# Linear attention with half of its key products moved to GpSimd, and cosine keys one step after their turning

## The chip, the core and the metric

The kernel runs on one core of a Trainium2 chip. The core has five engines that run side by side and wait for each other through semaphores: TensorE (PE in the profile, its weight loads PEld), VectorE (DVE), ScalarE (ACT), GpSimd (POOL) and SyncE (SP), which here issues DMAs. Each engine works off its own instructions in a fixed order. Tiles lie in SBUF or in PSUM; TensorE writes to PSUM, and GpSimd's operands in this kernel are all in SBUF. The metric is the device time of one execution in microseconds (us), the median of several runs.

## The reference, cut to what matters

The model has two layers of three blocks each, on x of 4 sequences x 512 positions x 256 channels, all in float32. Two blocks matter here. Cosine attention (16 heads of 128, one key and value head shared by all):

```python
xn = _layernorm(x, g_norm)
q = xn @ Wq
kv = xn @ Wkv
k, v = (kv[..., :DIM_HEAD], kv[..., DIM_HEAD:])
...
k = _l2norm(k)
...
sim = jnp.einsum('bhid,bjd->bhij', q, k)
attn = jax.nn.softmax(sim.astype(jnp.float32), axis=-1).astype(sim.dtype)
out = jnp.einsum('bhij,bjd->bhid', attn, v)
```

and gated linear attention (16 heads, 8 key channels and 16 value channels each):

```python
def step(S, inp):
    qt, kt, vt, gt = inp
    S = S * jnp.exp(gt)[..., None] + kt[..., None] * vt[..., None, :]
    ot = jnp.einsum('bhk,bhkv->bhv', qt, S)
    return (S, ot)
...
_, o = jax.lax.scan(step, S0, (qT, kT, vT, gT))
...
o = o * jax.lax.rsqrt(jnp.mean(o * o, axis=-1, keepdims=True) + EPS) * norm_w
o = o * (g * jax.nn.sigmoid(g))
return o.reshape(b, t, vd) @ Wo
```

## The kernel before, in words

The blocks follow each other, with parts of neighbouring blocks woven in. TensorE's order is that of the source; the order on the other engines was made when the program was built, by a planner that places each engine's instructions in advance.

**Cosine attention** (`cos`, some 537 to 1310 us of the span) goes over 16 batches, four heads of one sequence each, and within a batch over four steps k. Step k of batch n holds two `scores` (8 matmuls and an exponential), `values` (8 matmuls, a copy of the result, and the sum of the exponentials, part of it on GpSimd, line 726), and, at fixed (n, k), the preparation of what comes next. The next sequence is prepared by `enter`: at (1, 3) its layer norm, and at (2, 1) both `turned` (8 transposes on TensorE, then two scaled copies by VectorE, line 605, into `own_xt`) and, straight after, `keys` (16 matmuls on `own_xt`, then copies and the norm of the keys). At step (3, 1) of the same sequence the keys are transposed (`turn`, line 635).

**Linear attention** (`gla_stage`, `run`, some 1313 to 1490 us) lays out each state on partitions: one partition for a key channel of a head, time along the row. So the recurrence over time is one scan instruction of VectorE per value channel, with the decay as the factor. For a sequence b and a step n of four (`steps`, 16 in all), `states` handles two pairs of value channels, pair 0 and 1. For a pair:

- TensorE spreads the values over the partitions into `pv`, a PSUM tile of two banks with two buffers (line 932);
- VectorE multiplies by the keys in place, in PSUM (line 933, the *key product*);
- VectorE scans each half into `st` in SBUF (line 936), reading decay from SBUF and product from PSUM;
- GpSimd multiplies by the queries into another SBUF tile, `sq` (line 941, the *query product*); only the very last one of the stage is VectorE's.

`reads`, held back by one step, sums the query products over the key channels on TensorE (line 951) into an accumulator `po`, one for every two steps; there are two accumulator buffers in this stage. When one is complete, ScalarE squares it (959) and copies it to SBUF (963), and after the second GpSimd multiplies both by the gate (965). For the last sequence VectorE multiplies the accumulator by the gate directly (961). `output` then makes the norm and projects.

Woven into the stage are the preparation of the next sequence (`prepare`), the last feed-forward block (`extra`: a chain of small VectorE instructions, lines 517 to 540), and the folding of later weights (1087 to 1119), whose vectors GpSimd prepares (1063 to 1079) when their DMA has landed.

Of the kernel before, what the change touches and what calls it, by code (L numbers as in the profile page):

```python
# [9 lines left out]
F32 = mybir.dt.float32  # L10
I32 = mybir.dt.int32
U32 = mybir.dt.uint32
AF = mybir.ActivationFunctionType
ALU = mybir.AluOpType
AX = mybir.AxisListType

P = 128
# [8 lines left out]
class Model:  # L26
# [559 lines left out]
    def cos(self, w, woven):  # L586
# [4 lines left out]
        with self.pool("cos_2", 2) as p2:  # L591

            def normed(b):
                if b == 0:
                    return self.xn_first
                xn = p2.tile([P, NI, D], F32, name="cxn", tag="cxn", bufs=1)
                self.doubly(xn, b)
                return xn

            def turned(xn):  # L600
                xt = p2.tile([P, NC, T], F32, name="own_xt", tag="own_xt")

                def gained(dst, pt):
                    for c in range(NC):
                        nc.vector.tensor_scalar_mul(dst[:, c, :], pt[:, c, :], w["gn"][:, c : c + 1])

                self.turned(xn, xt, gained)
                return xt
# [33 lines left out]
                    self.b, self.h0 = n // NB, n % NB * 4  # L642

            bs = [Batch(n) for n in range(B * NB)]
            seq = {}

            def project(t, pair):
# [120 lines left out]
            def enter(b, part):  # L768
                if part == 0:
                    seq[b] = {"xn": normed(b)}  # L770
                else:
                    s = seq[b]
                    s["xt"] = turned(s["xn"])
                    s["k"], s["v"] = keys(s["xt"])

            if True:
                enter(0, 0)
                enter(0, 1)
                project(bs[0], 0)
                project(bs[0], 1)  # L780
                query_norms(bs[0])
                seq[0]["kt"] = turn(seq[0]["k"])
                project(bs[1], 0)
                project(bs[1], 1)
                spread_rows(bs[0].rn, bs[0].q)
                for n, t in enumerate(bs + [None]):
                    nxt, then = (bs[n + d] if n + d < len(bs) else None for d in (1, 2))
                    prev = bs[n - 1] if n else None
                    for k in range(4):
                        if prev and t and k == 0:  # L790
                            sums(prev)
                        if t:
                            scores(t, k, 0)
                            scores(t, k, 1)
                        if t and t.b + 1 < B and (n % NB, k) in ((1, 3), (2, 1)):
                            enter(t.b + 1, k == 1)
                        if n and nxt and k == 0:
                            project(nxt, 1)
                        if then and k == 3:
                            project(then, 0)  # L800
                        if nxt and k == 1 and nxt.h0 == 0:
                            seq[nxt.b]["kt"] = turn(seq[nxt.b]["k"])
                        if prev and not t and k == 1:
                            sums(prev)
                        if prev and k == 2:
                            if t:
                                scaled(prev.o, prev.wide, t.put)
                            else:
                                spread_rows(prev.rd, prev.o)
                        if t:  # L810
                            values(t, k)
                        if nxt and k == 0:
                            query_norms(nxt)
                        if nxt and k == 2:
                            scaled(nxt.q, nxt.sq, t.put)
                        if prev and k == (2 if t else 3):
                            output(prev)
                        if (n, k) in woven:
                            next(woven[n, k], None)
# [27 lines left out]
    def gla_stage(self, w):  # L847
# [64 lines left out]
        def run(order, extra, p2, p3):  # L912
# [9 lines left out]
            def states(b, n, pair):  # L922

                s = seqs[b]
                c, odd = n // 2, n % 2
                q = s.qk[:, 0, :].unsqueeze(1).to_broadcast([P, 2, T])
                k = s.qk[:, 1, :].unsqueeze(1).to_broadcast([P, 2, T])
                pv = self.st()
                for m in range(2):
                    r = pair * 2 + m  # L930
                    g = slice(r * 32, (r + 1) * 32)
                    nc.tensor.matmul(pv[:, m, :], lhsT=rep[g, odd, :], rhs=s.v[g, c, :], start=True, stop=True)
                nc.vector.tensor_tensor(pv, pv, k, op=ALU.mult)  # L933
                st = p3.tile([P, 2, T], F32, name="gs", tag="gs", bufs=3)
                for m in range(2):
                    s.scan = nc.vector.tensor_tensor_scan(  # L936
                        st[:, m, :], s.dec, pv[:, m, :], 0.0, op0=ALU.mult, op1=ALU.add
                    )
                sq = p3.tile([P, 2, T], F32, name="gqs", tag="gqs", bufs=4)
                end = (b, n, pair) == (order[-1], NB - 1, 1)  # L940
                (nc.vector if end else nc.gpsimd).tensor_tensor(sq, st, q, op=ALU.mult)
                return sq

            def reads(b, n, qs):
                s = seqs[b]
                c, odd = n // 2, n % 2
                if odd == 0:
                    s.po = s.po if c else []
                    s.po.append(self.ps())
                for r in range(4):  # L950
                    nc.tensor.matmul(
                        s.po[c][r * 32 : (r + 1) * 32, :], lhsT=summ[:, odd, :], rhs=qs[r // 2][:, r % 2, :],
                        start=odd == 0, stop=odd == 1,
                    )
                if odd:
                    if c == 0:
                        s.sq = p2.tile([P, NC, T], F32, name="gsq", tag="gsq", bufs=1)
                        s.o = p2.tile([P, NC, T], F32, name="go", tag="go")
                    nc.scalar.activation(s.sq[:, c, :], s.po[c], AF.Square)
                    if b == order[-1]:  # L960
                        nc.vector.tensor_tensor(s.o[:, c, :], s.po[c], s.g[:, c, :], op=ALU.mult)
                        return
                    nc.scalar.activation(s.o[:, c, :], s.po[c], AF.Copy)
                    if c:
                        nc.gpsimd.tensor_tensor(s.o, s.o, s.g, op=ALU.mult)

            def output(b, part):
                s = seqs[b]
# [27 lines left out]
            for n, (k, m) in enumerate(steps):  # L996
                b = order[k]
                nxt = order[k + 1] if k + 1 < len(order) else None
                prev = order[k - 1] if k else None
                qs = [states(b, m, 0)]  # L1000
                if nxt is not None:
                    prepare(nxt, {0: "turned", 1: 1, 2: 2, 3: 3}[m], p2)
                if m == 1 and k > 1:
                    with self.tc.issue_after(seqs[b].scan.ins):
                        output(order[k - 2], 2)
                qs.append(states(b, m, 1))
                for g in extra.get(n, ()):
                    next(g, None)
                if m == 0:
# [990 lines left out]
```

## Time and profile before

| | |
|---|---|
| median of 3 runs | 1987.21 us (1987.01 to 1987.48) |
| the profiled execution's own time | 1987.09 us |
| its span, first to last instruction | 1985.2 us |
| busy, whole span | PE 93%, DVE 62%, ACT 41%, POOL 36% |
| mean granted TensorE clock | 0.98 |
| first and last scan (line 936) | 1319.7 and 1467.6 us |
| first and last query product on POOL (line 941) | 1322.2 and 1463.9 us |

The costliest groups on the page with a part in the change are these (line, engine, operation, output from input, shapes and count; then busy us, mean ns of one; then idle us before them and who ended it):

```profile
L726 POOL TENSOR_TENSOR e<-e 128x1024 f32<-128x1024 f32 x64 | 155.6, 2430 | 598.8 <-ACT e L718 591.5
L253 PE MATMUL ps_two<-cq,ckt 128*128 128x512 f32 x512 | 236.6, 605 | 2.5 <-DVE cq L676 2.5
L253 PE MATMUL ps_acc<-e,cv 128*128 128x512 f32 x512 | 230.7, 593 | 1.8 <-ACT e L718 1.8
```

An instruction on a line of the timeline has its start, its duration, its engine and line, and in brackets the idle time of its engine before it with what ended that. Names say where a tile lies: those with `ps_` are in PSUM, all others in SBUF.

### The profile page before, as it was taken

How to read it: one execution, taken by the hardware profiler on the slowest of the kernel's cores; microseconds unless marked ns; L12 is line 12 of the kernel's file. 1: busy time of each engine (PE TensorE's matmuls, PEld its weight loads, DVE VectorE, ACT ScalarE, POOL GpSimd, SP SyncE). 2: the span in 40 equal slices, each digit the busy share in tenths (PEclk: the TensorE clock that was granted, in tenths of full speed). 3: DMA queues.
4: the chain of work that ended last, by engine and by line, in shares of the span. 5: the costliest groups of instructions: out<-in, count | busy, mean ns of one | idle time of the engine just before them, and what ended most of it. 6: DMA issues, size and time to landing. Idle time of an engine off the chain costs nothing.

```text
span 1985.2 us, 25536 instructions
## 1 busy us (share of the span) xinstructions
PE 1853.3 (93%) x8718; PEld 1057.8 (53%) x8718; DVE 1230.8 (62%) x2998; ACT 806.7 (41%) x1939; POOL 705.8 (36%) x710
## 2 busy tenths in 40 slices
PE   7999999999999999999999999978988869999886
PEld 4656566565644544544454554533346645666465
DVE  5676767767546546654755475278885566567454
ACT  3544545546333222323232224224423346666543
POOL 3554454544212113211321221236653235553232
PEclk9999999999999999999999999989989989999998
DMA  5020000000001112112111211110000000000001
GB/s 192 1 99 1 1 1 1 0 1 1 22 21 43 43 44 56 46 40 50 47 44 47 55 43 39 26 50 0 1 6 22 1 1 1 1 1 1 1 1 43
DMA packets 42880, 54.34 MB, mean 27 GB/s; under 512 B 12512, under 2 KB 25344, under 8 KB 42368
## 3 DMA queue, kind: packets, MB, share of 16 engines
q1 hardware_dynamic: 42752, 52.73, 10.0%
q8 instruction: 69, 1.13, 0.2%
q14 instruction: 59, 0.48, 0.1%
HBM read 19.14 MB, written 2.10 MB: 11 GB/s over the span
## 4 chain that ended last, share of the span: by engine, by line
PE 76%; DVE 13%; ACT 6%; POOL 2%; issue 2%; DMA 1%; SPq 0%; DVEq 0%; ACTq 0%; POOLq 0%
PE ps_acc L253 30%; PE ps_two L253 24%; PE ps_acc L1626 4%; PE ps_acc L446 3%; PE ps_acc L434 3%; DVE gs L936 2%; PE ps_acc L1673 2%; PE ps_acc L665 1%; PE ps_acc L1307 1%; ACT ws_junk L1352 1%; DVE ps_st L933 1%; DVE rp L161 1%; DVE ln_st L189 1%; PE ps_acc L1582 1%; DMA s16a<-in_mla_wqn 1%
## 5 line engine op out<-in xcount | busy, mean ns | idle before, releaser
L726 POOL TENSOR_TENSOR e<-e 128x1024 f32<-128x1024 f32 x64 | 155.6, 2430 | 598.8 <-ACT e L718 591.5
L271 DVE CUSTOM_DVE_ANT_0 ps_acc<-ps_acc,mask 128x128 f32<-128x128 f32 (+3 forms) x448 | 224.9, 540 | 63.6 <-PE ps_acc L1626 42.7
L718 ACT ACTIVATE e<-ps_two 128x1024 f32<-128x1024 f32 x128 | 130.5, 1021 | 292.8 <-PE ps_two L253 292.6
L253 PE MATMUL ps_two<-cq,ckt 128*128 128x512 f32 x512 | 236.6, 605 | 2.5 <-DVE cq L676 2.5
L253 PE MATMUL ps_acc<-e,cv 128*128 128x512 f32 x512 | 230.7, 593 | 1.8 <-ACT e L718 1.8
L417 POOL TENSOR_TENSOR prob<-prob,psum_row 128x256 f32<-128x256 f32 (+3 forms) x128 | 159.9, 1252 | 174.2 <-DVE psum_row L416 151.1
L412 ACT ACTIVATE prob<-ps_acc,nmax 128x128 f32<-128x128 f32 (+3 forms) x256 | 134.3, 528 | 152.8 <-DVE nmax L271 109.6
L253 PE MATMUL ps_acc<-key,q 128*128 128x256 f32 (+3 forms) x512 | 163.3, 441 | 5.9 <-POOL q L341 5.0
L253 PEld LDWEIGHTS ps_two<-cq,ckt 128*128 128x128 f32 x512 | 95.4, 192 | 130.0 <-issue 125.1
L253 PEld LDWEIGHTS ps_acc<-e,cv 128*128 128x128 f32 x512 | 96.5, 190 | 122.9 <-issue 96.9
L253 PE MATMUL ps_two<-own_xt,s16a 128*128 128x512 f32 x256 | 114.8, 592 | 0.0
L253 PE MATMUL ps_two<-s16b,cot 128*128 128x256 f32 x512 | 113.1, 379 | 0.0
L727 DVE TENSOR_TENSOR es<-e 128x512 f32<-128x512 f32 x64 | 43.9, 686 | 110.5 <-POOL e L726 110.5
L724 DVE COPY cot<-ps_acc 128x512 f32<-128x512 f32 x64 | 44.1, 689 | 104.7 <-PE ps_acc L253 104.7
L253 PEld LDWEIGHTS ps_two<-s16b,cot 128*128 128x128 f32 x512 | 97.3, 190 | 20.1 <-issue 7.7
L253 PEld LDWEIGHTS ps_acc<-key,q 128*128 128x128 f32 x512 | 83.2, 191 | 39.2 <-issue 16.9
L434 PEld LDWEIGHTS ps_acc<-ident,prob 128*128 128x128 f32 x640 | 76.6, 142 | 47.3 <-issue 37.4
L341 POOL TENSOR_TENSOR q<-rope,rope 64x512 f32<-64x512 f32 x64 | 81.1, 1267 | 49.7 <-DVE rope L338 47.0
L434 PE MATMUL ps_acc<-ident,prob 128*128 128x128 f32 x640 | 91.1, 274 | 3.8 <-ACT prob L412 2.7
L1626 PE MATMUL ps_acc<-lo_t 32*128 32x128 f32 (+3 forms) x512 | 87.1, 454 | 3.2 <-ACT lo_t L1586 3.2
L446 PE MATMUL ps_acc<-prt,kv 128*64 128x384 f32 (+3 forms) x512 | 78.4, 439 | 4.8 <-DVE prt L129 4.6
L1626 PE MATMUL ps_acc<-lo_qm,lo_t 32*128 32x384 f32 (+3 forms) x512 | 80.9, 451 | 0.7 <-DVE lo_qm L1664 0.7
(470 smaller groups left out, 3494.4 us busy)
## 6 DMA issues: line engine op xcount, KB each, us to landing
csq<-crn SPq DMA_DIRECT2D x240, 64.0 KB, 2.0
es<-crd SPq DMA_DIRECT2D x240, 64.0 KB, 2.0
x<-in_x SPq DMA_DIRECT2D x4, 512.0 KB, 7.6
s16b<-in_mla_wo SPq DMA_DIRECT2D x1, 2048.0 KB, 17.9
s16a<-in_cos_wq SPq DMA_DIRECT2D x1, 2048.0 KB, 9.1
s16b<-in_cos_wo SPq DMA_DIRECT2D x1, 2048.0 KB, 8.5
out_x<-x SPq DMA_DIRECT2D x4, 512.0 KB, 2.9
s16a<-in_mla_wqn SPq DMA_DIRECT2D x1, 1536.0 KB, 12.8
```

Of the source, the lines that this page charges most:

```text
L253: self.nc.tensor.matmul(out, lhsT=l, rhs=r, start=k == 0, stop=k == n - 1)
L271: return self.nc.vector.tensor_tensor_reduce(out=sc[:, :n], in0=sc[:, :n], in1=self.mask[:, T - n :], scale=-1.0, scalar=3.0e38, op0=ALU.a ...
L341: nc.gpsimd.tensor_tensor(dst[k][r], t1[r], t3[r], op=ALU.add)
L412: nc.scalar.activation(pr[:, k, :n], sc[k][:, :n], AF.Exp, bias=nm[:, k : k + 1], scale=-1.0, accum_out=sm[:, k : k + 1],)
L417: nc.gpsimd.tensor_tensor(pr[:, :, :n], pr[:, :, :n], sm.unsqueeze(2).to_broadcast([P, 2, n]), op=ALU.mult)
L434: nc.tensor.transpose(pt[:, k, keys], pr[:, k0 + k, keys], self.ident)
L446: nc.tensor.matmul(po[k * R : (k + 1) * R, j * P :], lhsT=s.kv[:, j, 0, :], rhs=prt[:, k, j, j * P :], start=j == 0, stop=j == NI - 1,)
L718: nc.scalar.activation(t.e[:, pair * 2 : pair * 2 + 2, :], sc, AF.Exp)
L724: t.put = nc.vector.tensor_copy(t.o[:, k, :], po)
L726: nc.gpsimd.tensor_tensor(e2, t.e[:, 0:2, :], t.e[:, 2:4, :], op=ALU.add)
L727: nc.vector.tensor_tensor(t.es[:, k, :], e2[:, 0, :], e2[:, 1, :], op=ALU.add)
L1626: nc.tensor.matmul(sc[:, col : col + n], lhsT=left, rhs=right, start=True, stop=True)
```

## The change

In cosine attention, `enter` is split in three: the layer norm at (1, 3), the turning at (2, 1), and the key projection at (2, 2), one step later. In linear attention, pair 1 of each step, except in the very last step, takes another way: ScalarE copies the spread values from PSUM into the SBUF tile `st`, GpSimd multiplies them there by the keys, and VectorE scans `st` in place. Pair 1 is issued ahead of pair 0. The query product is written in place, so `sq` is gone, and `st` has 7 buffers where the two tiles had 3 and 4. In all sequences VectorE now multiplies the accumulator by the gate straight from PSUM; ScalarE's copy and GpSimd's gate product are gone.

```diff
@@ cosine attention
+            ENTER = [(1, 3), (2, 1), (2, 2)]
...
             def enter(b, part):
                 if part == 0:
                     seq[b] = {"xn": normed(b)}
+                elif part == 1:
+                    seq[b]["xt"] = turned(seq[b]["xn"])
                 else:
                     s = seq[b]
-                    s["xt"] = turned(s["xn"])
                     s["k"], s["v"] = keys(s["xt"])
...
                 enter(0, 1)
+                enter(0, 2)
...
-                        if t and t.b + 1 < B and (n % NB, k) in ((1, 3), (2, 1)):
-                            enter(t.b + 1, k == 1)
+                        if t and t.b + 1 < B and (n % NB, k) in ENTER:
+                            enter(t.b + 1, ENTER.index((n % NB, k)))
@@ linear attention, states
-                nc.vector.tensor_tensor(pv, pv, k, op=ALU.mult)
-                st = p3.tile([P, 2, T], F32, name="gs", tag="gs", bufs=3)
+                end = (b, n) == (order[-1], NB - 1)
+                st = p3.tile([P, 2, T], F32, name="gs", tag="gs", bufs=7)
+                if pair == 0 or end:
+                    nc.vector.tensor_tensor(pv, pv, k, op=ALU.mult)
+                else:
+                    nc.scalar.copy(st, pv)
+                    nc.gpsimd.tensor_tensor(st, st, k, op=ALU.mult)
+                    pv = st
                 for m in range(2):
                     s.scan = nc.vector.tensor_tensor_scan(
                         st[:, m, :], s.dec, pv[:, m, :], 0.0, op0=ALU.mult, op1=ALU.add
                     )
-                sq = p3.tile([P, 2, T], F32, name="gqs", tag="gqs", bufs=4)
-                end = (b, n, pair) == (order[-1], NB - 1, 1)
-                (nc.vector if end else nc.gpsimd).tensor_tensor(sq, st, q, op=ALU.mult)
-                return sq
+                end = end and pair == 0
+                (nc.vector if end else nc.gpsimd).tensor_tensor(st, st, q, op=ALU.mult)
+                return st
@@ reads
-                    if b == order[-1]:
-                        nc.vector.tensor_tensor(s.o[:, c, :], s.po[c], s.g[:, c, :], op=ALU.mult)
-                        return
-                    nc.scalar.activation(s.o[:, c, :], s.po[c], AF.Copy)
-                    if c:
-                        nc.gpsimd.tensor_tensor(s.o, s.o, s.g, op=ALU.mult)
+                    nc.vector.tensor_tensor(s.o[:, c, :], s.po[c], s.g[:, c, :], op=ALU.mult)
@@ the steps of run
-                qs = [states(b, m, 0)]
+                qs = [states(b, m, 1)]
...
-                qs.append(states(b, m, 1))
+                qs.insert(0, states(b, m, 0))
```

## The prediction

> **What bounds the kernel now.** I read the busy shares first, then two stretches side by side, then the waits inside them, and last single instructions. TensorE (PE) has 93% of the whole span, but that is an average over stages.
>
> ```profile
> 520.00:1000.00 480.00, 471.41 (x1455) 240.40 (x1452) 267.93 (x457) 136.32 (x187) 105.59 (x43) 1.00 0.18 42
> 1320.00:1471.00 151.00, 130.67 (x490) 49.18 (x490) 137.81 (x182) 58.64 (x93) 104.36 (x85) 0.89 0.04 9
> ```
>
> Each line gives length, then busy time of PE, weight loads, VectorE (DVE), ScalarE (ACT), GpSimd (POOL), and PE's clock. The first stretch is cosine attention: PE 98% busy, so every PE idle counts there. The second is linear attention: DVE has 137.8 of 151 us and leads, PE 130.7 at clock 0.89, POOL 104.4. The two halves of the change fall in these two stages.
>
> ```profile
> L936 DVE TENSOR_TENSOR_SCAN gs<-gdec,ps_st 128x512 f32<-128x512 f32 x48 | 56.1, 1207 | 1.8
> L933 DVE TENSOR_TENSOR ps_st<-ps_st,gqk 128x1024 f32<-128x1024 f32 x24 | 29.2, 1217 | 4.4 <-PE ps_st L932 4.4
> L941 POOL TENSOR_TENSOR gqs<-gs,gqk 128x1024 f32<-128x1024 f32 x23 | 54.3, 2359 | 24.1 <-DVE gs L936 21.4 <-PE ps_st L932 2.0 <-DVE f_n L164 0.6
> L965 POOL TENSOR_TENSOR go<-go,gg 128x1024 f32<-128x1024 f32 x3 | 7.1, 2360 | 0.0
> ```
>
> Each pair of head groups costs DVE one key product (1.22) and two scans (2.33 for both, they overlap by 0.08); POOL follows with a query product of 2.36 and mostly waits for DVE. Notice the operands: scan and key product read one tile from PSUM (ps_st) and one from SBUF. POOL reads two from SBUF. Now look at what happens elsewhere when DVE, too, reads two tiles from SBUF:
>
> ```profile
> 776.09 2.35 POOL L726 TENSOR_TENSOR e<-e 128x1024 f32<-128x1024 f32 x1 [11.43 <-ACT e L718]
> 776.14 2.32 DVE L161 TENSOR_TENSOR rp<-rp,ln_rstd 128x4 f32<-128x4 f32 x1 [1.43 <-ACT ln_rstd L160]
> ...
> 992.00 2.35 DVE L693 TENSOR_TENSOR cot<-cot,es 128x1024 f32<-128x1024 f32 x2
> 993.05 4.12 POOL L726 TENSOR_TENSOR e<-e 128x1024 f32<-128x1024 f32 x1 [3.87 <-ACT e L718]
> 994.27 0.69 DVE L727 TENSOR_TENSOR es<-e 128x512 f32<-128x512 f32 x1
> ```
>
> At 776.14 a DVE product of 128x4 elements, elsewhere 0.16 us, takes 2.32: it ends when POOL's product ends (778.44). At 993.05 it is the other way: POOL's product, elsewhere 2.35, takes 4.12, for it gets nothing until DVE's chain of such products ends at 994.96. In linear attention, L161 at 1325.79 takes 1.71 inside a POOL product. The two engines exclude each other, whole instructions at a time. The scans of today, with PSUM under one operand, run inside POOL's products at 1.2 us all 64 times (1186 to 1222 ns): no exclusion.
>
> **Cosine part.** Keys now come one step after the turning. Today PE transposes and waits at once for DVE's copy of the result:
>
> ```profile
> 845.94 1.04 PE L230 MATMUL ps_two<-ident,cxn 128*128 128x128 f32 x8
> 849.76 3.87 PE L253 MATMUL ps_two<-s4a,own_xt 128*128 128x256 f32 x16 [2.78 <-DVE own_xt L605]
> ```
>
> Three sequences show it, at 662.75 (0.94), 849.76 (2.78) and 1036.76 (2.78); the first sequence's 0.95, at 536.88, is not touched. In the new order a values group (3.44) and a scores group (3.43) of PE lie between, 6.9 us, where the worst case needs 2.8 (its whole start-to-start is 3.8, 1.0 of it the transposes). Saved: 0.94 + 2.78 + 2.78 = **6.5 us**, bounds 0 to 6.5. If that cover failed, the 2.78 would come back. Late next are the keys, about 7 us later: PE turns them some 47 us after today's projection (710.08 after 662.75), so 40 stay. No instruction or DMA is added.
>
> **Linear attention, DVE and ACT.** Of 16 pairs with the higher index, 15 lose their key product on DVE: 15 x 1.22 = 18.3 off. Six gate products come over (the last sequence's two are there already), by row L961 at 0.69: 4.1 on. DVE goes from 137.8 to 123.6. ACT gets 15 copies PSUM to SBUF at 1.01 (row L903, same shape) and loses six at 0.59: 58.6 + 15.2 - 3.5 = 70 of 151 us, hidden; if it were not, each copy would stand 1.0 us before its POOL product. The gate product reads the accumulator on DVE, so one of two accumulators is held until DVE gets there; I cost that at nothing while DVE has slack, at 0.7 each (4 us) if not.
>
> **Linear attention, POOL.** 15 key products in place, 128x1024 (in-place row L965: 2.36): 35.4 on. Three gate products off: 7.1. POOL goes from 104.4 to 132.7 and passes DVE.
>
> **The new operand.** The 30 scans of these pairs now read decay and product both from SBUF. No row shows such a scan. Below: they run like today's, 1.17 each at no cost to POOL; a gain by SBUF I leave out, since the DVE copy L724 from PSUM (0.69) and the SBUF product L727 (0.69) of the same size cost the same. Above: they exclude POOL like every two-SBUF product did, 15 x 2.33 = 35.0 us taken from POOL. The nearest rows, L693 and L161, are of the same engine and operands, so I take the upper end.
>
> The Trainium skill, page "SBUF — State Buffer", section "Who interferes with whom", states the same as a rule: a DVE instruction with two SBUF inputs contends with a GpSimd instruction that reads SBUF, and whoever starts second blocks fully. It names tensor_tensor, not the scan. It speaks against this change: by it the time is the main sum below, without it the first rival's.
>
> **The sum goes by POOL's queue.** Its first key product can run before the queue stops, as today, for a DMA:
>
> ```profile
> 1320.70 0.86 POOL L1066 TENSOR_SCALAR r_ws_ob<-r_ws_ob 128x256 f32<-128x256 f32 x1 [30.05 <-DMA r_ws_ob<-in_ws_ob]
> ...
> 1387.07 2.35 POOL L941 TENSOR_TENSOR gqs<-gs,gqk 128x1024 f32<-128x1024 f32 x1 [6.54 <-DVE gs L936]
> ```
>
> From 1320.70: 132.7 - 2.4 = 130.3 of work, 35.0 blocked by scans, and 6.5 for the hole before 1387.07, where DVE works through a chain of 15 small instructions of the feed-forward layer; the new order has the next scans behind that chain too. 171.8, so POOL ends at 1492.5. Today the recurrence ends with DVE's last query product:
>
> ```profile
> 1469.83 1.22 DVE L941 TENSOR_TENSOR gqs<-gs,gqk 128x1024 f32<-128x1024 f32 x1
> ```
>
> at 1471.05, whereupon PE sums and gates. 1492.5 - 1471.05 = **21.4 us later**. The tail after it is the same.
>
> Profiled execution: span 1985.2, time 1987.09, so 1.9 around it; the three timed runs have a median of 1987.21, 0.1 apart. 1985.2 - 6.5 + 21.4 + 1.9 = **2002.0 us**. Its own range: 1995 if the scans fill the hole of 6.5; 2014 if POOL's other waits today (ACT chains of 0.6 to 1.7 us, some 6 us in all) and DVE's other two-SBUF instructions (about 6 us) come on top.
>
> **Rivals.** (1) *The scan does not exclude POOL* (other side, faster). Then POOL has 130.3, the hole 6.5, and idle where a pair's query product stands right behind its key product in POOL's queue as built and must wait for the scan between: four steps at 2.4, four with 1.3 of other work between at 1.1. 130.3 + 6.5 + 9.7 + 4.4 = 150.9, end 1471.6, 0.5 later than now: 1987.1 - 6.5 + 0.5 = 1981. It decides as soon as fewer than 20 of the 35.0 us block (21.4 - 6.5 = 14.9 too many). For it: no scan with SBUF alone is in the trace. Against: no two-SBUF product of DVE that began inside one of POOL's products ended before it. (2) *DVE's load alone sets the stage* (faster): 18.3 - 4.1 = 14.2 saved, with 6.5 gives 1966. Against it is POOL's 132.7 before any wait, and PE's 130.7. (3) *DVE suffers most*: every one of the 30 scans waits for a POOL product of 2.36, 70.8 on DVE: 123.6 + 70.8 = 194.4 against 137.8 busy of 151; idle kept, that is 43 to 57 later, less 6.5: 2024 to 2037. Against: back-to-back DVE instructions keep POOL out (992.00 to 994.96), so the second scan of a pair should not wait. (4) *The cosine part does nothing* and the rest goes as the main case: 2008; inside its range.
>
> **Chances.** Main 0.70 (2002, own range 1995 to 2014), with (4) in it; (1) 0.14; (2) 0.07; (3) 0.09. A measurement here can tell 0.2%, 4 us, from no change. Faster by more: 0.12 of (1), the 0.07 of (2), 0.01 of the main case's lower tail: 0.20. Within: 0.02 of (1), 0.03 of the main case: 0.05. Slower: the rest, 0.75. The range runs from 1977, below (1), to 2020, above the main case's end; (2) and most of (3) are left out.
>
> **What would show it.** In the changed profile: the waits of PE for own_xt at the three later sequences gone; POOL the busiest engine of linear attention or nearly so, with products of 2.36 stretched to 3.5 or 4.7 where they begin beside an SBUF scan, and SBUF scans of more than 1.2 us where they begin inside a POOL product; PSUM scans unchanged at 1.2; the stage some 21 us longer, with lower PE share. I am wrong if SBUF scans keep 1.2 us while POOL's products beside them keep 2.36: then rival (1). I am also wrong on the sum if POOL's queue stands idle for something else, such as ACT's copies or the accumulator held for a gate product.

## The result, and the profile after

The changed kernel takes 2023.29 us, the median of four runs (2022.04 to 2024.94), against 1987.26 for the kernel before (1987.01 to 1987.48). The ratio is 1.0182, with a 95% interval of 1.0164 to 1.0199. The change costs 36 us. The prediction was 2002, with a range of 1977 to 2020: right in sign, too low by 21 us. The profiled execution took 2023.34 us, of which the span is 2021.2.

The cosine part first. In the waits of PE within cosine attention, the kernel before has "PE ps_two L253 <- DVE own_xt L605" with 7.4 us in 4 waits. The same view of the changed kernel (us in total, number of waits, the longest) has only the first sequence's left:

```profile
PE ps_two L253 <- DVE own_xt L605: 1.0, 1, 1.0
```

The last add of cosine attention starts at 1299.55 us, where it started at 1308.59. Of these 9.0 us, 0.7 were there already before the edit first acts, so the part gained 8.3.

Linear attention lost more than this. From the start of that add to the end of VectorE's last query product it takes 203.3 us, where it took 162.5: 40.9 more. These are its largest groups on VectorE and GpSimd in the changed kernel, other engines left out (line, engine, operation, output from input, shapes, count; busy us, mean ns; idle us before them and who ended it). `s16a` holds decay, queries and keys of the first sequence, `gdec` and `gqk` those of the later ones:

```profile
L949 POOL TENSOR_TENSOR gs<-gs,gqk 128x1024 f32<-128x1024 f32 x23 | 55.6, 2423 | 30.0 <-DVE gs L945 26.6 <-DVE ln_mv L190 3.4
L945 DVE TENSOR_TENSOR_SCAN gs<-gdec,gs 128x512 f32<-128x512 f32 x22 | 31.4, 1464 | 26.9 <-POOL gs L942 26.9
L945 DVE TENSOR_TENSOR_SCAN gs<-gdec,ps_st 128x512 f32<-128x512 f32 x26 | 30.1, 1200 | 0.2
L942 POOL TENSOR_TENSOR gs<-gs,gqk 128x1024 f32<-128x1024 f32 x11 | 25.9, 2352 | 3.6 <-ACT gs L941 3.6
...
L945 DVE TENSOR_TENSOR_SCAN gs<-s16a,gs 128x512 f32<-128x512 f32 x8 | 17.0, 2165 | 1.6 <-POOL gs L942 1.6
...
L945 DVE TENSOR_TENSOR_SCAN gs<-s16a,ps_st 128x512 f32<-128x512 f32 x8 | 9.3, 1199 | 0.0
```

Scans that read their product from PSUM keep their 1.20 us. Those that read it from SBUF take 1.46 and 2.17 on average. The timeline of the changed kernel shows why (start us, us, engine, line):

```profile
1338.61 6.69 DVE L945 TENSOR_TENSOR_SCAN gs<-s16a,gs 128x512 f32<-128x512 f32 x2
1338.64 2.36 POOL L949 TENSOR_TENSOR gs<-gs,s16a 128x1024 f32<-128x1024 f32 x1
1340.94 3.27 POOL L942 TENSOR_TENSOR gs<-gs,s16a 128x1024 f32<-128x1024 f32 x1
```

Two scans, 2.33 us elsewhere, take 6.69 beside two GpSimd products, and the second product takes 3.27 instead of 2.35. But this is the smaller half of what there is to see. Seventy microseconds later:

```profile
1406.96 2.35 POOL L942 TENSOR_TENSOR gs<-gs,gqk 128x1024 f32<-128x1024 f32 x1
...
1409.35 2.34 DVE L945 TENSOR_TENSOR_SCAN gs<-gdec,gs 128x512 f32<-128x512 f32 x2 [7.84 <-POOL gs L942]
1411.83 2.35 POOL L949 TENSOR_TENSOR gs<-gs,gqk 128x1024 f32<-128x1024 f32 x1 [2.52 <-DVE gs L945]
```

VectorE stands 7.84 us for GpSimd's key product, then GpSimd stands 2.52 for VectorE's scans. The waits of the whole stage (1311 to 1503 us) say how much there is of this:

```profile
POOL gs L949 <- DVE gs L945: 30.1, 14, 5.4
DVE gs L945 <- POOL gs L942: 28.5, 9, 7.8
```

The busy times of the stage, in the changed kernel (window, its length, busy us and instructions of PE, PEld, DVE, ACT, POOL, granted clock of PE, DMA share, GB/s):

```profile
1311.40:1502.00 190.60, 139.37 (x482) 52.23 (x480) 140.74 (x176) 69.15 (x101) 141.35 (x96) 0.83 0.03 7
```

GpSimd is busy for 141.4 us, some 11 of which are its instructions held up beyond their usual time (an estimate, against the lower quartile of each operation and shape in the stage), and not busy for 49.3 of 190.6. In the kernel before, the same reading (1320.6 to 1471.0) gives 104.4 busy and 46.0 not busy of 150.4. So GpSimd got 37 us of work and held-up time, the stage got 40 us longer, and GpSimd's empty time stayed. The prediction had left 6.5 us of it.

### The profile page after: what moved, and what is told of

It reads as the page before. It is cut to its first block, busy times and chain, and to the rows that moved or that the text cites. A ratio compares the mean times of both kernels' runs of the same rounds, so it can differ in the third digit from the quotient of the medians.

```text
span 2021.2 us, 25521 instructions
## 1 busy us (share of the span) xinstructions
PE 1866.6 (92%) x8718; PEld 1063.7 (53%) x8718; DVE 1236.3 (61%) x2989; ACT 818.8 (41%) x1948; POOL 745.7 (37%) x722
## 4 chain that ended last, share of the span: by engine, by line
PE 72%; DVE 14%; ACT 6%; POOL 4%; issue 2%; DMA 1%; SPq 0%; DVEq 0%; ACTq 0%; POOLq 0%
PE ps_acc L253 29%; PE ps_two L253 22%; PE ps_acc L1629 4%; PE ps_acc L446 3%; DVE gs L945 3%; PE ps_acc L434 3%; PE ps_acc L1676 2%; PE ps_acc L666 1%; POOL gs L949 1%; PE ps_acc L1310 1%; ACT ws_junk L1355 1%; POOL gs L942 1%; DVE ln_st L189 1%; DVE rp L161 1%; DVE ps_acc L271 1%
## 5 line engine op out<-in xcount | busy, mean ns | idle before, releaser
L271 DVE CUSTOM_DVE_ANT_0 ps_acc<-ps_acc,mask 128x128 f32<-128x128 f32 (+3 forms) x448 | 224.9, 540 | 63.7 <-PE ps_acc L1629 42.7
L253 PE MATMUL ps_two<-cq,ckt 128*128 128x512 f32 x512 | 235.2, 602 | 2.5 <-DVE cq L677 2.5
L253 PE MATMUL ps_acc<-e,cv 128*128 128x512 f32 x512 | 230.8, 593 | 1.9 <-ACT e L719 1.8
L253 PE MATMUL ps_acc<-key,q 128*128 128x256 f32 (+3 forms) x512 | 163.6, 442 | 5.8 <-POOL q L341 5.0
L253 PEld LDWEIGHTS ps_two<-cq,ckt 128*128 128x128 f32 x512 | 94.8, 191 | 128.9 <-issue 124.1
L253 PEld LDWEIGHTS ps_acc<-e,cv 128*128 128x128 f32 x512 | 96.3, 190 | 122.0 <-issue 96.2
L253 PE MATMUL ps_two<-own_xt,s16a 128*128 128x512 f32 x256 | 114.8, 592 | 0.0
L253 PE MATMUL ps_two<-s16b,cot 128*128 128x256 f32 x512 | 113.1, 379 | 0.0
L728 DVE TENSOR_TENSOR es<-e 128x512 f32<-128x512 f32 x64 | 43.9, 686 | 111.9 <-POOL e L727 111.9
L253 PEld LDWEIGHTS ps_two<-s16b,cot 128*128 128x128 f32 x512 | 97.3, 190 | 20.1 <-issue 7.7
L253 PEld LDWEIGHTS ps_acc<-key,q 128*128 128x128 f32 x512 | 83.4, 191 | 39.5 <-issue 17.1
## 6 DMA issues: line engine op xcount, KB each, us to landing
s16a<-in_cos_wq SPq DMA_DIRECT2D x1, 2048.0 KB, 10.6
```

The lines of the kernel that those rows point to most:

```text
L253: self.nc.tensor.matmul(out, lhsT=l, rhs=r, start=k == 0, stop=k == n - 1)
L271: return self.nc.vector.tensor_tensor_reduce(out=sc[:, :n], in0=sc[:, :n], in1=self.mask[:, T - n :], scale=-1.0, scalar=3.0e38, op0=ALU.a ...
```

## The experiments

The runs, each with its ratio to the kernel before on the same chip:

| run | what it is | us | ratio (95% interval) |
|---|---|---|---|
| cos_only | cosine part alone | 1978.91 | 0.9954 (0.9937 to 0.9971) |
| cos_gate | cosine part, gate product from PSUM | 1980.59 | 0.9961 (0.9945 to 0.9976) |
| scan_sbuf | cos_gate, pair 1 scanned from SBUF | 2002.83 | 1.0073 (1.0058 to 1.0088) |
| quarter | 7 key products on GpSimd, not 15 | 2005.99 | 1.0076 (1.0058 to 1.0094) |
| changed kernel | | 2023.29 | 1.0182 (1.0164 to 1.0199) |
| ahead | key product a step early | 2021.68 | 1.0166 (1.0151 to 1.0181) |
| k_first | and ahead of the query products | 2030.01 | 1.0199 (1.0182 to 1.0216) |
| pair0_first | pair 0 issued first | 2023.41 | 1.0168 (1.0142 to 1.0194) |
| ps_back | ahead, product copied back to PSUM | 2023.54 | 1.0166 (1.0145 to 1.0187) |
| dec_sbuf | fewer banks, decay copied in SBUF | 2034.48 | 1.0225 (1.0210 to 1.0240) |
| dec_psum | the same, decay copied into PSUM | 2039.15 | 1.0248 (1.0232 to 1.0263) |
| kf_dec_sbuf | order of k_first, decay in SBUF | 2057.96 | 1.0338 (1.0322 to 1.0353) |
| kf_dec_psum | order of k_first, decay in PSUM | 2025.83 | 1.0174 (1.0157 to 1.0191) |
| load_psum | cos_gate, 15 more GpSimd products | 2012.01 | 1.0123 (1.0108 to 1.0138) |
| load_sbuf | scan_sbuf, 15 more GpSimd products | 2022.33 | 1.0175 (1.0158 to 1.0192) |
| chains_gate | cos_gate, short chains on VectorE | 2005.17 | 1.0081 (1.0064 to 1.0097) |
| chains_load | load_psum, the same | 2014.67 | 1.0131 (1.0116 to 1.0146) |
| chains_after | changed kernel, the same | 2018.99 | 1.0153 (1.0136 to 1.0170) |

### The parts of the change, one by one

**cos_only** is the kernel before with the edits to `ENTER` and `enter`, and nothing else of the diff.

> The kernel before with the cosine part of the change alone (turning and keys/values one entry apart); linear attention as before. In the trace of the changed kernel the last add of cosine attention ends at 1299.55 where it ended at 1308.59, so the theory that the cosine part is worth more than the prediction's 6.5 us expects the whole 9.0 to reach the end: 1978 us, between 1977 and 1980. The prediction's own size expects 1980 to 1981. If linear attention gives the gain back (it starts earlier but waits for something else), 1985 to 1988.

Measured 1978.9. By its ratio that is 9.1 us off (5.8 to 12.5). The cosine part's gain reaches the end; the interval is too wide to tell its size from 6.5.

**cos_gate** takes the gate's part of the diff as well:

```diff
-                    if b == order[-1]:
-                        nc.vector.tensor_tensor(s.o[:, c, :], s.po[c], s.g[:, c, :], op=ALU.mult)
-                        return
-                    nc.scalar.activation(s.o[:, c, :], s.po[c], AF.Copy)
-                    if c:
-                        nc.gpsimd.tensor_tensor(s.o, s.o, s.g, op=ALU.mult)
+                    nc.vector.tensor_tensor(s.o[:, c, :], s.po[c], s.g[:, c, :], op=ALU.mult)
```

> The kernel before with the cosine part and with the gate product read from PSUM by VectorE for every sequence; all key products stay on VectorE. It takes 7.1 us off GpSimd and 3.5 us off ScalarE and puts 4.1 us on VectorE. If VectorE sets the pace of linear attention (prediction's reading of before), it is up to 4 us slower than the cosine part alone: 1978 to 1983. If GpSimd's queue sets it, up to 4 us faster: 1974 to 1978. Either way the gate part is not where the changed kernel's 36 us went, so far under 2000.

Measured 1980.6. The intervals of the two overlap: the gate part by itself moves nothing that this measurement can tell. The loss lies in what the diff does to pair 1: its key products, the place that its scans read, and the order.

**scan_sbuf** adds to this the change of place alone. VectorE still makes every key product:

```diff
+                to = st if pair and (b, n) != (order[-1], NB - 1) else pv
-                nc.vector.tensor_tensor(pv, pv, k, op=ALU.mult)
+                nc.vector.tensor_tensor(to, pv, k, op=ALU.mult)
+                pv = to
```

> As the run before this (cosine part, gate product from PSUM, all key products on VectorE), and only this beside it: VectorE writes the key product of pair 1 into SBUF rather than back into PSUM, so that its 30 scans read decay and product both from SBUF, as they do in the changed kernel. No work moves to GpSimd. Theory that such scans and GpSimd's instructions shut each other out: the 30 scans stretch (13.4 us over their 1.2 us in the changed kernel) and GpSimd waits 15 x 2.33 = 35 us within its 41 us of idle time, so 8 to 20 us above the run before this, with single scans over 2 us. Theory that the place of the operand costs nothing and the whole loss of the changed kernel is waiting between the engines: within 2 us of the run before this, scans at 1.19 to 1.22 us.

Measured 2002.8: 22 us above cos_gate, just over the 8 to 20 of the first theory, for 30 operands that moved from PSUM to SBUF. In the groups of its linear attention the operand decides the duration, on one engine and in one stage:

```profile
L941 DVE TENSOR_TENSOR_SCAN gs<-gdec,gs 128x512 f32<-128x512 f32 x22 | 36.8, 1714 | 0.2
L941 DVE TENSOR_TENSOR_SCAN gs<-gdec,ps_st 128x512 f32<-128x512 f32 x26 | 30.4, 1205 | 0.8
```

The first rival of the prediction (such scans don't exclude GpSimd) is out.

**quarter** is the changed kernel with `if pair == 0 or end or n % 2 == 0:`, so that 7 products move rather than 15.

> The changed kernel, with pair 1's key product on GpSimd only in odd steps (7 products rather than 15; in even steps VectorE makes it in PSUM, and its scans read PSUM). Between none of them (cosine part and gate from PSUM: 1980.6) and 15 of them (2023.3) it should lie in proportion to the scans from SBUF if each such scan costs by itself: 1980.6 + 42.7 x 7/15 = 2000.5, between 1996 and 2005. If GpSimd's whole load is what decides (it has over 50 us free in linear attention without the key products, and 7 of them with their blocked scans take 33), it costs next to nothing: 1978 to 1986.

Measured 2006.0, 25.4 of the 42.7 us between cos_gate and the changed kernel, for 7 of 15 products (20 by proportion; by the ratios it is 22.9 of 43.9). It lies just above the range by proportion, and far from the 1978 to 1986 of the other theory: the first seven products are not free.

### Is it the order? Four runs

**ahead** issues the next step's spread, copy and key product of pair 1 one step early:

```diff
-                qs = [states(b, m, 1)]
+                qs = [states(b, m, 1, made)]
...
+                if n + 1 < len(steps):
+                    k2, m2 = steps[n + 1]
+                    made = product(order[k2], m2)
```

> The changed kernel with one thing moved: the spread of pair 1, its ScalarE copy and its GpSimd key product are issued one step early, so that VectorE's scan of pair 1 should not stand waiting for GpSimd. Same instructions on every engine. Theory that the loss beyond the prediction is the loop (GpSimd key product, VectorE scans behind it in order, GpSimd query products waiting for those scans): VectorE's 28.5 us of waits for the key product and most of GpSimd's 30.1 us for scans go, and the end moves to GpSimd's queue as predicted, 1997 to 2008. Theory that exclusion between scans and GpSimd is the whole loss: little changes, 2018 to 2025. Theory that nothing but waits costs: 1975 to 1985.

Measured 2021.7: no better. But the trace shows that the waits it was to remove are still there, for the early product now stood behind a query product in GpSimd's queue, which waits for VectorE:

```profile
DVE gs L960 <- POOL gs L943: 31.6, 9, 5.8
POOL gs L964 <- DVE gs L960: 31.3, 15, 5.2
```

**k_first** therefore puts it ahead of both query products on GpSimd, by an order given in the program (`issue_after` the key product around the query product).

> The changed kernel, with the key product of the next step one step early, as in the run 'ahead', and now also put ahead of both query products of this step in GpSimd's queue (in 'ahead' it still stood behind a query product that waits for VectorE's scan, and VectorE's waits for it stayed at 31.6 us). Same instructions on every engine. Theory that the excess over the prediction is GpSimd standing idle because of the order (in the changed kernel 30.2 of 191.6 us pass in which neither GpSimd nor an SBUF scan runs; the prediction had 6.5): most of it goes, 1998 to 2008. Theory that the order is not the point, and SBUF scans and GpSimd shutting each other out sets the time however they are ordered: 2016 to 2024.

Measured 2030.0, which neither theory had, and this time most of the waits did go: VectorE's for the key product from 31.6 to 10.4 us. What came in their place is exclusion, in the same groups of its linear attention:

```profile
L962 DVE TENSOR_TENSOR_SCAN gs<-gdec,gs 128x512 f32<-128x512 f32 x22 | 52.4, 2421 | 8.9 <-POOL gs L945 8.9
L962 DVE TENSOR_TENSOR_SCAN gs<-gdec,ps_st 128x512 f32<-128x512 f32 x26 | 30.0, 1198 | 0.2
```

When scans no longer wait for the product in front of them, they meet the next GpSimd instruction and wait for that.

**pair0_first** undoes the diff's swap: `qs = [states(b, m, 0)]`, then pair 1.

> The changed kernel with one part of its edit undone: pair 0, whose key product VectorE makes in PSUM, is issued before pair 1 in each step (and VectorE's last query product is that of pair 1). Theory that a good part of the 20.5 us between 'scan_sbuf' (2002.8) and the changed kernel is VectorE standing at pair 1's scan with pair 0's work queued behind it: that work now goes first, while GpSimd makes the product, so 2005 to 2018. Theory that GpSimd's in-order queue only turns the same round trip about (its query product of pair 0 goes first, its key product of the next step later): 2020 to 2030.

Measured 2023.4. VectorE waits longer for the key product (43.2 us), GpSimd longer for the scans (36.7). The swap neither helped nor hurt.

**ps_back** is 'ahead', with ScalarE copying the product back to PSUM, so that no scan has two operands in SBUF:

```diff
                 nc.gpsimd.tensor_tensor(st, st, k, op=ALU.mult)
-                return st, st
+                nc.scalar.copy(pv, st)
+                return st, pv
```

> The run 'ahead' with one instruction more per key product on GpSimd: ScalarE copies the product back into the PSUM buffer that its spread came from, and pair 1's scans read it there, so that no scan reads two operands from SBUF; 15 copies of about 1.0 us on ScalarE, which is busy for 70 of 190 us. Theory that the exclusion of SBUF scans and GpSimd is worth over 20 us ('scan_sbuf' and the pair with the decay in PSUM: 22 and 32): scans at 1.2 us and a time of 1985 to 2008, in spite of the longer way. Theory that the round trip over ScalarE and GpSimd sets the time and is now longer: 2018 to 2040.

Measured 2023.5. All 64 scans are back at 1.20 us, and the time has not moved. VectorE waits 27.6 us for the copies and GpSimd 32.5 for the scans. So exclusion is enough to lose these microseconds (scan_sbuf), but taking it away by this longer way does not get them back.

### Exclusion by itself

The decay is the scans' other operand. Two runs differ only in where a copy of it lies. To free a PSUM bank, pair 0 has one buffer, and pair 1's spreads go through one bank, half by half:

```diff
-            with m.psum("ps_g", st=2, two=1, acc=2)
+            with m.psum("ps_g", st=1, two=1, acc=2, half=1, dec=1)
...
+                if n == 0 and pair:
+                    s.dec1 = self.ps("dec")        (dec_sbuf: an SBUF tile)
+                    nc.scalar.copy(s.dec1, s.dec)
```

> Control for the next run. The changed kernel, with one PSUM buffer of two banks for pair 0 rather than two buffers shared by both pairs, one bank for the spreads of pair 1, which ScalarE copies out half by half, and a ScalarE copy of the decay into another SBUF tile once a sequence, which pair 1's scans read. Both theories: near the changed kernel or somewhat above, since PE has fewer banks: 2022 to 2040.

> As its control, with one difference: the copy of the decay lies in a PSUM bank, so that pair 1's 30 scans read only the product from SBUF. Same instructions, same order of work. Theory that two SBUF operands shut GpSimd out (and GpSimd the scans): pair 1's scans fall to 1.2 us each, overlap GpSimd's products, and the time is 18 to 40 us below the control, under 2005. Theory that the loss is waiting in the loop between ScalarE, GpSimd and VectorE: within 5 us of the control.

Measured 2034.5 and 2039.2: no gain, against the expectation. With these banks VectorE waits 42 and 50 us for the key product, and the scans hardly meet GpSimd (their mean is 1224 and 1208 ns). The planner's order on GpSimd is also not quite the same in the two. But where scans and GpSimd do meet, the timelines show the mechanism, at the same place in both. First dec_sbuf, whose scans have two SBUF operands:

```profile
1501.93 2.36 DVE L951 TENSOR_TENSOR_SCAN gs<-gd,gs 128x512 f32<-128x512 f32 x2
1502.07 1.12 POOL L203 TENSOR_SCALAR ln_off<-ln_off 128x4 f32<-128x4 f32 x1
1503.16 2.19 POOL L990 TENSOR_TENSOR grs<-grs,grp 128x512 f32<-128x512 f32 x1
```

and dec_psum, with the decay in PSUM:

```profile
1504.54 2.31 DVE L951 TENSOR_TENSOR_SCAN gs<-ps_dec,gs 128x512 f32<-128x512 f32 x2
1504.68 0.22 POOL L203 TENSOR_SCALAR ln_off<-ln_off 128x4 f32<-128x4 f32 x1
1504.87 1.27 POOL L990 TENSOR_TENSOR grs<-grs,grp 128x512 f32<-128x512 f32 x1
```

The small GpSimd instruction takes 1.12 us beside an SBUF scan and 0.22 beside the other; the larger one 2.19 and 1.27. Each waits for a whole scan.

Then the same pair in the order of k_first, in which scans and products do meet (the spread of pair 0 goes ahead of pair 1's in both):

> Control for the next run: the order of the run 'k_first' (key product one step early and ahead of the query products), with the PSUM layout of 'dec_sbuf' (one two-bank buffer for pair 0, one bank for pair 1's spreads, the decay copied into another SBUF tile once a sequence). With the loop between GpSimd and VectorE opened, the SBUF scans meet GpSimd's products, as they did in 'k_first': scans of over 2 us, 2020 to 2040. Both theories below expect this.

> As its control, with the copied decay in a PSUM bank; the same instructions in the same order. Theory of two bounds side by side (the loop in which VectorE and GpSimd wait for each other's results, and the exclusion of SBUF scans and GpSimd; taking away one alone moves nothing since the other then sets the time): here both are away, so the scans stay at 1.2 us beside GpSimd's products and the time falls 20 to 45 us below the control, to 1980 to 2005. Theory that a third thing sets the time (the copies on ScalarE, PE's banks and clock, GpSimd's own work): within 8 us of the control.

Measured 2058.0 and 2025.8: 32 us apart, with the same instructions in the same order on VectorE and GpSimd. The groups of pair 1's scans, first with the decay in SBUF (kf_dec_sbuf):

```profile
L972 DVE TENSOR_TENSOR_SCAN gs<-gd,gs 128x512 f32<-128x512 f32 x30 | 82.8, 2799 | 7.7 <-POOL gs L950 7.7
```

then in PSUM (kf_dec_psum):

```profile
L972 DVE TENSOR_TENSOR_SCAN gs<-ps_dec,gs 128x512 f32<-128x512 f32 x30 | 35.0, 1208 | 23.4 <-POOL gs L950 23.4
```

The 32 us bear out the second half of the expectation; its absolute time (1980 to 2005) does not come, since the scarce banks cost waits of their own (VectorE stands 23.6 us behind the spreads through one bank).

### GpSimd's load by itself

Neither order nor exclusion had explained the last 20 us, so two runs gave GpSimd as much work as the change does, with results that nobody reads:

```diff
+                if pair and (b, n) != (order[-1], NB - 1):
+                    more = p3.tile([P, 2, T - 16], F32, name="gmore", tag="gmore", bufs=1)
+                    with self.tc.issue_after(read.ins):
+                        nc.gpsimd.tensor_tensor(more, k[..., 16:], q[..., 16:], op=ALU.mult)
```

> The run 'cos_gate' (1980.6; every scan reads its product from PSUM) with 15 products of 128x992 more on GpSimd, each behind the query product of pair 1, which write to a tile that nobody reads: some 15 x 2.28 = 34 us of work for GpSimd that no engine waits for. GpSimd is idle for 50 of 150 us there, so by a sum of its queue alone: 1980 to 1988. If it comes out much higher, GpSimd's load itself delays its query products, and PE and the reads behind them.

> The run 'scan_sbuf' (2002.8; pair 1's scans read decay and product from SBUF) with the same 15 products more on GpSimd. GpSimd then has the work of the changed kernel and the same exclusion, but VectorE never waits for it. Theory that GpSimd's queue of work and blocked time sets the end, as the prediction summed it: near the changed kernel, 2014 to 2026. Theory that the round trip (VectorE standing for GpSimd's key product) is what the last 20.5 us are: 2002 to 2010.

load_psum took 2012.0, 31 us above cos_gate: against the expectation, and the most telling miss of the study. The added products are 34.4 us of work, and cost 31, on an engine that had 54 us free. The window of the stage in cos_gate:

```profile
1311.40:1462.00 150.60, 131.04 (x490) 49.35 (x490) 139.04 (x187) 55.78 (x87) 96.82 (x81) 0.89 0.03 9
```

and of load_psum:

```profile
1311.40:1492.00 180.60, 137.85 (x486) 52.67 (x488) 142.52 (x186) 55.78 (x87) 129.75 (x96) 0.81 0.03 7
```

GpSimd is not busy for 150.6 - 96.8 = 53.8 us in the one and 180.6 - 129.8 = 50.9 in the other. Here its empty time did not take up the work. VectorE, which was idle for 12 us, now waits 27.4 for the spreads of PE (from 4.9), and PE's granted clock in the window falls from 0.89 to 0.81. Nor does "nobody" hold beyond the results: at 1317.88 VectorE's small product on L161, elsewhere 0.16 us, takes 1.75 beside an added product.

load_sbuf took 2022.3, the time of the changed kernel within 1 us, though VectorE reads none of GpSimd's added products there. So 15 more GpSimd products and 30 scans from SBUF are together enough for the changed kernel's loss; alone they cost 31 and 22 us, together 42. That VectorE has 15 products fewer in the changed kernel bought nothing that shows in the time.

PE's waits in load_psum pointed at one road by which the load travels (us in total, number, longest):

```profile
PE ps_two L230 <- ACT xn L213: 11.5, 2, 5.9
PE ps_acc L253 <- POOL grs L983: 11.3, 2, 5.7
```

In cos_gate PE does not wait for `xn` in this stage, and little for `grs`:

```profile
PE ps_acc L253 <- POOL grs L979: 1.2, 1, 1.2
```

These waits grew by 21.6 us. Between the two windows PE's idle time grew by 23.2 (from 19.6 to 42.8) and its busy time, at the lower clock, by 6.8; that is the 30.0 us. Both waits are for ends of chains of short GpSimd instructions (a layer norm's and the heads' reciprocal root) that stand behind products of 2.35 us. But the planner also placed them anew. The first layer norm's chain, from its first instruction on GpSimd to its `ln_rstd`, in cos_gate:

```profile
1318.30 0.19 POOL L141 TENSOR_SCALAR rp<-ln_mv 128x4 f32<-128x4 f32 x1
...
1321.12 0.20 POOL L148 TENSOR_TENSOR ln_rstd<-ln_rstd,rp 128x4 f32<-128x4 f32 x1
```

and in load_psum:

```profile
1320.14 0.19 POOL L141 TENSOR_SCALAR rp<-ln_mv 128x4 f32<-128x4 f32 x1
...
1341.82 0.21 POOL L148 TENSOR_TENSOR ln_rstd<-ln_rstd,rp 128x4 f32<-128x4 f32 x1
```

In cos_gate no product stands between the two. In load_psum four query products and two added ones do. So the 31 us of load_psum hold two things, the added work and a new order of the old, and the two load runs do not separate them.

Three runs move these chains to VectorE (`eng = nc.vector`, and the layer norm without the argument that puts its root on GpSimd):

> Control: 'cos_gate' (1980.6) with the two chains of short instructions that GpSimd does for the sequences beside the recurrence (layer norm's reciprocal root of two sequences, and the heads' root behind grs of three) on VectorE. VectorE sets the pace there, and gets some 10 us of work: 1985 to 1995.

> 'load_psum' (2012.0) with the same chains on VectorE. Theory that the added products cost time because these chains stand behind them and PE stands for the chains: PE's 22.8 us of waits for grs and xn go, and the cost of the added products falls from 31 us to under 14, so 1990 to 2004. Theory that the added products delay the query products, and with them the whole loop: the cost stays at 25 us or more, 2010 to 2022.

> The changed kernel (2023.3) with the same chains on VectorE, which is idle for 50 of 190 us there; it also takes 16 us of work off GpSimd. Theory of the chains: 2000 to 2012. Theory that the query and key products themselves and the exclusion set the time: 2015 to 2028.

The control lost far more than expected (2005.2, 25 us above cos_gate). With the chains moved, the same added products cost 9.5 us instead of 31. That is under the 14 of the theory of the chains, while the time itself, 2014.7, lies in the other theory's range. GpSimd's empty time fell there from 89.4 us (chains_gate, 1311.4 to 1481) to 63.8 (chains_load, 1311.4 to 1492.3): most of the added work did go into it. It fits the road, but a cost can also hide behind the control's own new waits; PE still waits 11.7 us for xn in chains_load, after 10.7 in chains_gate. The changed kernel gained 4 us (6 by the ratios, whose intervals overlap), where the theory of the chains had 11 to 23. These runs don't settle it.

## Why the prediction was wrong in size

**The cosine part** was right in kind: the three waits went, no new ones came. Its size was 6.5 us, and the runs gave 8.3 (the trace) to 9.1 (the ratio of cos_only). The step counted the waits alone. The keys' matmuls behind the three waits had also been slower, 3.86, 3.87 and 5.16 us for the 16, and take 3.62 without a wait: 2.0 us that were left out, and with them it is 8.5. Behind the third wait the granted clock of PE was 0.79 (1036.70 to 1044.00), and in the changed kernel it is 1.00 there.

**The loads** came as worked out: ScalarE 69.2 us against 70, hidden; VectorE 140.7, less the 13.4 by which the SBUF scans were held up 127.3, against 123.6; PSUM scans 1.20. GpSimd's work without held-up time is 130 against 130.3. The gate product on VectorE was costed at nothing while VectorE has slack, and cos_gate bears this out within what can be measured.

**The new operand** was the right mechanism, taken at the upper bound for a good reason: the scans do exclude GpSimd. By itself it costs 22 us. It agrees with what the prediction cited from the Trainium skill ("SBUF — State Buffer", "Who interferes with whom"), and the runs with the decay in PSUM show the other half of that rule, too: with one SBUF operand fewer the scan neither waits (1208 ns in kf_dec_psum) nor makes GpSimd wait (0.22 us in dec_psum against 1.12 in dec_sbuf). One reading behind it was too broad: of the 64 scans of before, 36 overlap a GpSimd product, not all. As none of them is longer than 1222 ns, the conclusion stands.

**The step that failed is "The sum goes by POOL's queue"**: 130.3 of work, 35.0 blocked, and 6.5 for one hole. Measured are 130 of work, some 11 held up, and 49.3 in which GpSimd is not busy. The blocked time was put too high: at 1409.35 the two SBUF scans run while GpSimd waits for them anyway, so they block nothing. The empty time was far too low: 6.5 against 49.3. From GpSimd's first work behind its early key product to VectorE's last query product it is 191.4 us (1311.5 to 1502.9) against the 171.8 of the sum: 19.6 too few, nearly the whole error of the forecast. The sum treated the empty time of before (46.0 us) as room which the new work would fill, once GpSimd had the most work. But GpSimd sits in a loop: its query products wait for VectorE's scans, PE's sums and the next spreads come after them, and the scans after those, every engine in its own fixed order. In cos_gate, quarter, the changed kernel, load_psum and load_sbuf its empty time was 53.8, 57.9, 49.3, 50.9 and 48.3 us, while its busy time went from 96.8 to 143.4. That this loop is what keeps the time empty is argued from the waits, and no run shows it by itself; the empty time is no fixed amount either, as chains_gate and chains_load show (89.4 and 63.8).

**The tail** was taken to be the same, and was 4.2 us longer (518.3 us from VectorE's last query product to the end, after 514.1). It lies in the first stretch behind linear attention. The window of the first 29 us there, in the kernel before:

```profile
1471.00:1500.00 29.00, 25.02 (x106) 15.61 (x110) 18.60 (x58) 12.28 (x28) 10.99 (x16) 0.95 0.15 46
```

and in the changed kernel:

```profile
1502.90:1531.90 29.00, 25.54 (x95) 15.41 (x96) 18.51 (x57) 11.98 (x27) 11.01 (x16) 0.85 0.14 46
```

PE's granted clock is 0.85 there, not 0.95, and 0.93 in the next 60 us, not 1.00. In 'ahead', whose stage is as long as the changed kernel's, the clock is 0.95 and 1.00 there, and matching instructions come as early as in the kernel before, within 0.2 us, from 32 us behind VectorE's last query product to 200. With the 19.6 of the sum, less the 2.7 us by which GpSimd's work began earlier than the 6.5 allowed for (1311.46 against 1320.70 - 6.5), that makes 21.1 of the 21.3 us between 2002.0 and 2023.3.

**The rivals.** (1) is out by scan_sbuf. (2), VectorE's load alone, is out: 15 products fewer on VectorE bought nothing. (3) gave 2024 to 2037, and the result lies just below, but not for its reason: it had every SBUF scan waiting for a product of 2.36, 70.8 us, and the scans were held up by 13.4 in all. Only the order of k_first brought its mechanism about (k_first and kf_dec_sbuf). (4) is out by cos_only.

What stays open is by which link GpSimd's load delays the end: the short chains and the place that the planner gives them, the query products, or PE's lower clock. In the changed kernel PE is idle for 51.2 us of the stage, after 19.6 in cos_gate. Of its waits 10.6 us are for the chains (1.2 in cos_gate), 9.0 for GpSimd's query products (none) and 11.0 for scans that still hold the spreads' banks (6.2). So the chains are a part at most there.

The lowest median of the study is that of cos_only: 1978.9 us, 0.46% (0.29 to 0.63) below the kernel before and 44 us below the changed one. cos_gate (1980.6) can't be told from it.

## What to carry to other kernels

An engine's empty time is not room for more work just because it is empty. Where the engine waits for others in every turn of a loop, added work can come back in the time at nearly its full length (31 us for 34.4 in load_psum) or at less (9.5 for the same products in chains_load). Test it by a load whose results nobody reads, and look at whether the planner kept the order of the rest. Before moving an operand of a VectorE instruction from PSUM to SBUF, look at whether GpSimd works beside it and the other operand is in SBUF already: here the move cost 22 us before any work had changed engine. Try the parts of a change alone: one of these was worth 9 us, and was buried under the loss of the others.

## What the runs showed of the hardware

A scan with decay and product both in SBUF shuts out GpSimd's smallest instructions too: 128x4 elements took 1.12 us beside it and 0.22 beside a scan with the decay in PSUM. A second scan right behind the first can lose to GpSimd, against the prediction's reading of the chain at 993.05: at 1338.61 two scans and two products took turns, and the scans needed 6.69 us for 2.33. Two ways of losing can stand one behind the other: from ahead to k_first VectorE's waits for the key product fell by 21 us, the mean of the SBUF scans in the larger group rose from 1496 to 2421 ns, and the time rose by 8 us (7 by the ratios). A lower granted clock in a stage need not last beyond it: the changed kernel and 'ahead' both have 0.83 in linear attention, and behind it 0.85 and 0.95 in the first 29 us.
